# A graph-attention layer on one core: four ring buffers instead of five, and a twelfth weight kept in SBUF

## The chip, the core and the metric

The kernel runs on one core of one Trainium2 chip. Its time is the device time of one execution in microseconds (us). The kernel before took 2680.55 us, the median of three runs (2680.24 to 2683.42). One more execution was profiled; all rows below come from it.

## What is computed

The reference is one attention layer over 128 graphs of 128 nodes with 768 features, in float32, with 12 heads of 64:

```
h = relu(layernorm(x))                      # x: (128, 128, 768)
q, k, v = h @ Wq + bq, h @ Wk + bk, h @ Wv + bv
s = q k^T / sqrt(64) + beta * adj           # per head, adj: (128, 128, 128)
s = where(adj > 0, s, -9e15)
out = x + softmax(s) v
```

Most of the arithmetic is the three projections, 768 x 768 each, over 16,384 rows.

## The kernel before, in words

**Groups and slices.** The work runs in 32 groups of four graphs (`GRP = 4`). A group has three slices, in this order: `qk0` (the first half of the columns of Wq and Wk), `v` (Wv), and `qk1` (the other half of Wq and Wk). In groups 1 to 31 a slice is not computed as plain block products: the blocks go through a fast matrix multiplication with 15 products (table `PRODUCTS`), and each product is again seven 128x128 products instead of eight. `product` (line 662) issues one of them: 7 zones, each in two column halves, 28 TensorE matmul records of line 679 in the trace and as many weight loads. So a group is 45 products. This text numbers them as **slots 0 to 44**: 0 to 14 are `qk0`, 15 to 29 are `v`, 30 to 44 are `qk1`. The order inside a slice is a written list (`ORDER`; group 1 and the last group have lists of their own). The scores (line 774) and the attention products (line 853) of earlier slices are put between the slots by a table of due times (`TABLE`), and so are the evictions and decodings on VectorE, ScalarE and GpSimd (`EVICT`, `DECODE`).

**Prepared weights.** Each slot multiplies with a prepared weight: sums and differences of weight blocks, a tile of 128 x 7 x 128 floats, 448 KB. The 45 prepared weights are the same for all groups. Eleven of them stay in SBUF as tiles named `res_...` (`RESIDENT`, line 119, gives their slots: 0, 3, 16, 17, 19, 28, 29, 35, 38, 39, 42). The other 34 are written to DRAM once (`kept_...`, line 387) and read back in every group from 1 to 31 into a ring of `RING = 5` buffers (tag `T`, tiles `T_qk`, `T_v`).

**The ring.** `load_T` (line 433) issues one read on SyncE's queue (SP). At the end of each streamed slot, `product` calls it once (line 683). It takes the buffer that this slot has just freed, so the DMA waits, on SP, for the slot's last matmul. With five buffers the read that waits for one streamed slot brings the weight of the fifth streamed slot after it. SP works in order: everything behind a waiting read waits too. The same queue carries the loads of x (`x`, `xo`, `sbig`), of `adj`, and the output.

**Group 0.** The first group has no prepared weights yet. `plain_slice` (line 1027) computes its slices with ordinary block products, from raw weights in `sbig`. Beside it `prepare` (line 365) makes the 45 prepared weights step by step: `sums` on VectorE, and `finish` with `rest` on VectorE and GpSimd, which ends with the store to DRAM. `home(name)` (line 367) chooses where a weight is made: in its own tile if it is resident; else, for `qk0` and `v`, by a running count (`made_in`): the counts 2, 5 and 7 of every eight go to a buffer of the tag `e` (three buffers, later used for the scores), the others to the ring's tag `T`. The non-resident weights of `qk1` all go to `T`. A buffer can be taken again only when its store has landed. The ring is then filled ahead of group 1: two `load_T` in the middle of the `qk1` preparation (line 417) and `RING - 2` more at lines 1316 and 1317.

**Blocks.** Eight more tiles `home0` to `home7` (line 644) hold projections while they are summed up. In group 0 the first six serve `qk0`; the other two are first written by the first row of `qk1`.

Of the kernel before, what the change touches and what calls it, by code (L numbers as in the profile page):

```python
# [11 lines left out]
F32 = mybir.dt.float32  # L12
# [6 lines left out]
P = 128  # L19
# [12 lines left out]
@with_exitstack  # L32
def kernel(
    ctx: ExitStack,
    tc: tile.TileContext,
    x: bass.AP,
    adj: bass.AP,
    wq: bass.AP,
    bq: bass.AP,
    wk: bass.AP,  # L40
    bk: bass.AP,
    wv: bass.AP,
    bv: bass.AP,
    beta: bass.AP,
    out: bass.AP,
):

    nc = tc.nc
    keep = ctx.enter_context(tc.tile_pool(name="keep", bufs=1))
    bad = keep.tile([1, 1], I32, name="bad")
    args = (x, adj, wq, bq, wk, bk, wv, bv, beta, out)
    direct(tc, *args, bad)
    again = nc.values_load(bad[0:1, 0:1])
    with tc.If(again > 0):
        general(tc, *args)  # L60
# [54 lines left out]
PORDER = (1, 0, 5, 2, 3, 10, 7, 6, 13, 11, 4, 9, 14, 8, 12)  # L115
XORDER = (1, 0, 5, 2, 3, 10, 6, 7, 13, 11, 4, 9, 14, 8, 12)
ORDER = {"qk0": (1, 0, 5, 2, 10, 3, 6, 7, 13, 11, 9, 4, 14, 12, 8), "v": (1, 0, 5, 2, 10, 3, 6, 7, 13, 11, 4, 9, 14, 8, 12), "qk1": (4, 1, 0, 8, 2, 3, 5, 6, 7, 10, 9, 13, 11, 12, 14)}
RING = 5
RESIDENT = (0, 3, 16, 17, 19, 28, 29, 35, 38, 39, 42)
EB = 3  # L120
HOMES = 8

# [103 lines left out]
def direct(ctx, tc, x, adj, wq, bq, wk, bk, wv, bv, beta, out, bad):  # L226
# [25 lines left out]
    const = ctx.enter_context(tc.tile_pool(name="const", bufs=1))  # L252
# [104 lines left out]
    sequence = [(sl, n) for sl in ("qk0", "v", "qk1") for n in ORDER[sl]]  # L357
    resident = {key: const.tile([P, 7, P], F32, name=f"res_{key[0]}_{key[1]}") for key in (sequence[at] for at in RESIDENT)}
    kept, tz = {}, {}
    made_in = [0]  # L360

    def quarters(t):
        return t[:, 0:6].rearrange("p (c z) n -> p c z n", c=2)[:, :, 0:2]

    def prepare(sl):

        def home(name):
            n = [i for i, p in enumerate(PRODUCTS) if p[1] == name][0]
            if (sl, n) in resident:
                return resident[sl, n]  # L370
            made_in[0] += sl != "qk1"
            if sl != "qk1" and made_in[0] % 8 in (2, 5, 7):
                t = work.tile([P, 2, W], F32, tag="e", name=f"prep_{sl}_{n}", bufs=EB)
                return t.rearrange("p i w -> p (i w)")[:, 0:7 * P].rearrange("p (z n) -> p z n", n=P)
            return work.tile([P, 7, P], F32, tag="T", name=f"prep_{sl}_{n}", bufs=RING)

        def rest(n, t, b11, b12, b22, b=None):
            nc.vector.tensor_tensor(t[:, 6], b12, b11, ALU.subtract)
            nc.vector.tensor_tensor(t[:, 2], b22, b12, ALU.add)
            if b is not None:  # L380
                nc.gpsimd.tensor_copy(t[:, 0:2], b[:, 0])
                nc.gpsimd.tensor_copy(t[:, 3], b[:, 1, 0])
            nc.gpsimd.tensor_tensor(t[:, 4], t[:, 1], t[:, 6], ALU.add)
            nc.gpsimd.tensor_tensor(t[:, 5], t[:, 0], t[:, 4], ALU.subtract)
            if (sl, n) not in resident:
                k = kept[sl, n] = dram.tile([P, 7, P], F32, name=f"kept_{sl}_{n}")
                nc.sync.dma_start(k, t)

        made = {}

        def sums(name):
            for out, a, b, sign in SUMS_B:
                if out == name:
                    if out not in made:
                        made[out] = home(out)
                    at = [quarters(made[q]) if q in made else wt[sl, q] for q in (a.strip("-"), b)]
                    op = ALU.add if sign > 0 else ALU.subtract
                    if a[0] == "-":
                        nc.vector.scalar_tensor_tensor(quarters(made[out]), at[0], -1.0, at[1], op0=ALU.mult, op1=op)
                    else:  # L400
                        nc.vector.tensor_tensor(quarters(made[out]), at[0], at[1], op)  # L401

        def finish(name):
            n = [i for i, p in enumerate(PRODUCTS) if p[1] == name][0]
            if name in made:
                t = made[name]
                rest(n, t, t[:, 3], t[:, 4], t[:, 1])
            else:
                t, b = home(name), wt[sl, name]
                rest(n, t, b[:, 1, 0], b[:, 1, 1], b[:, 0, 1], b)  # L410

        steps = []
        for first, then_finish in PREPARED:
            for name in first:
                steps.append(lambda name=name: sums(name))
            if sl == "qk1" and first[0] == "T0":
                steps += [load_T, load_T]
            for name in then_finish:
                steps.append(lambda name=name: finish(name))
        return steps  # L420
# [12 lines left out]
    def load_T():  # L433
        if nt[0] < len(ring):
            G, sl, n = ring[nt[0]]
            nt[0] += 1
            t = tz[G, sl, n] = work.tile([P, 7, P], F32, tag="T", name=f"T_{G}_{sl}_{n}", bufs=RING)
            nc.sync.dma_start(t, kept[sl, n])
# [202 lines left out]
        while between and next(between[0], None) is None:  # L641
            between.popleft()

    homes = deque(const.tile([P, 7, P], F32, name=f"home{i}") for i in range(HOMES))
    home_of = {}

    def home_qk(G, sl, r, j, zones=False):
# [542 lines left out]
    def then(at, f, *args):  # L1190
        todo.setdefault(at, []).append(lambda: f(*args))
# [6 lines left out]
    def bias(G, *at):  # L1198
        for n in at:
            then(n, bias_step, G)  # L1200
# [114 lines left out]
    bias(1, 4, 6, 8)  # L1315
    for n in range(2, RING):
        then(10 + n, load_T)
# [29 lines left out]
    while events:  # L1347
        _, _, f, args = heapq.heappop(events)
# [149 lines left out]
```

## Time and profile before

| what | value |
|---|---|
| median of three runs | 2680.55 us |
| profiled execution, its own time | 2681.86 us |
| its span, first to last instruction | 2680.1 us |
| granted TensorE clock, mean | 0.997 |
| busy share of the span: PE, VectorE, ScalarE, GpSimd | 99%, 81%, 66%, 78% |
| data moved by DMA | 721.95 MB, 269 GB/s on average |
| reads from the ring's DRAM copies | 744 + 310 = 1054 of 448 KB |

The busy share of PE counts pipelined matmuls whose ends are modelled, so what an idle stretch costs is read from the waits, the timeline and the chain of waits instead. In the timeline a row gives the start in us from the span's start, the length in us, the engine, the line of the kernel, the operation, what it writes and reads, its shape, and how many instructions are merged; a bracket gives the idle time before it and what ended it. A row of line 679 with x28 is one slot, with x56 two slots. In the view of waits a row gives who waited for whom, the sum in us, how often, and the longest. `issue` stands for a wait that no event in the profile explains.

### The profile page before, as it was taken

What the parts mean: (1) busy time and instruction counts of PE and PEld (TensorE: products, weight loads), DVE (VectorE), ACT (ScalarE), POOL (GpSimd) and SP (SyncE); (2) the same over time, 40 slices, a digit from 0 to 9 for tenths busy, and PEclk for the clock granted to TensorE, in tenths of its full rate; (3) what the DMA queues carried; (4) which work ended last, traced back from release to release, by engine and by line L of the source; (5) the groups of instructions that cost most, each with busy time, mean ns of one, the idle gap of its engine ahead of it and who ended that gap; (6) DMA issues with size and microseconds to landing.
All of it is one profiled execution on the core that took longest, in us unless ns stands there. A gap on an engine that the chain in (4) does not pass through costs nothing.

```text
span 2680.1 us, 121170 instructions
## 1 busy us (share of the span) xinstructions
PE 2648.6 (99%) x52041; PEld 2569.4 (96%) x52041; DVE 2180.8 (81%) x2702; ACT 1756.8 (66%) x4608; POOL 2095.4 (78%) x3043
## 2 busy tenths in 40 slices
PE   9999999999999999999999999999999999999998
PEld 8799999999999999999999999999999999999997
DVE  7878888878888888888788888788888778777886
ACT  2567766676766677666677666777666766657654
POOL 5877778877778877878777788777788777887775
PEclk9999999999999999999999999999999999999999
DMA  8799898899989989989989999898999889888875
GB/s 250 257 284 279 271 279 276 270 283 270 276 278 274 278 279 268 285 273 269 284 271 274 277 279 276 274 273 272 283 274 275 264 247 283 271 266 263 244 253 171
DMA packets 526962, 721.95 MB, mean 269 GB/s; under 512 B 105932, under 2 KB 370648, under 8 KB 526424
## 3 DMA queue, kind: packets, MB, share of 16 engines
q1 hardware_dynamic: 525776, 713.38, 87.6%
q8 instruction: 411, 6.73, 1.0%
q14 instruction: 127, 1.04, 0.1%
q10 hardware_dynamic: 648, 0.79, 0.1%
HBM read 647.99 MB, written 66.05 MB: 266 GB/s over the span
## 4 chain that ended last, share of the span: by engine, by line
PE 91%; DMA 3%; DVE 2%; ACT 1%; issue 1%; SPq 1%; POOL 0%; ACTq 0%; DVEq 0%
PE pair L679 78%; PE pair L774 7%; PE pair L853 6%; DMA x<-in_x_dram 1%; DMA T_qk<-kept_qk 1%; DMA sbig<-in_L_gnn_Wk_dram 1%; PE pair L1046 1%; DVE prep_qk L401 0%; SPq L334 0%; SPq L597 0%; ACT x L558 0%; DVE home L702 0%; DMA kept_qk<-prep_qk 0%; DVE e L787 0%; ACT sbig L521 0%
## 5 line engine op out<-in xcount | busy, mean ns | idle before, releaser
L702 DVE TENSOR_TENSOR home<-home,pair 128x896 f32<-128x896 f32 x824 | 870.7, 1076 | 201.2 <-PE pair L679 197.2
L679 PE MATMUL pair<-sbig,T_qk 128*64 128x128 f32 x13020 | 840.8, 273 | 2.4 <-DVE home L702 1.2
L679 PEld LDWEIGHTS pair<-sbig,T_qk 128*64 128x64 f32 x13020 | 712.2, 137 | 12.1 <-issue 6.8
L679 PE MATMUL pair<-A,T_qk 128*64 128x128 f32 x7812 | 521.2, 273 | 1.7 <-DMA T_qk<-kept_qk 1.0
L737 POOL TENSOR_TENSOR home<-home 128x256 f32<-128x256 f32 x301 | 241.5, 802 | 273.8 <-DVE home L702 273.6
L834 ACT ACTIVATE e<-e,sm 128x64 f32<-128x64 f32 x1512 | 381.4, 344 | 102.8 <-DVE sm L822 101.9
L679 PEld LDWEIGHTS pair<-A,T_qk 128*64 128x64 f32 x7812 | 429.9, 137 | 3.6 <-ACT home L724 1.4
L853 PE MATMUL pair<-v,e 128*64 128x65 f32 x6048 | 406.5, 221 | 0.0
L853 PEld LDWEIGHTS pair<-v,e 128*64 128x64 f32 x6048 | 365.0, 137 | 3.0
L679 PE MATMUL pair<-T_v,sbig 128*64 128x128 f32 x6076 | 365.3, 274 | 1.6 <-issue 1.0
L679 PEld LDWEIGHTS pair<-T_v,sbig 128*64 128x64 f32 x6076 | 340.0, 138 | 8.8 <-issue 8.0
L722 ACT ACTIVATE home<-pair 128x640 f32<-128x640 f32 x328 | 231.5, 706 | 117.5 <-PE pair L679 87.9
L740 POOL TENSOR_TENSOR home<-home 128x256 f32<-128x256 f32 x301 | 281.3, 934 | 23.6
L679 PE MATMUL pair<-sbig,res_qk 128*64 128x128 f32 x4340 | 287.6, 273 | 0.0
L738 POOL TENSOR_TENSOR home<-home 128x256 f32<-128x256 f32 x301 | 264.7, 879 | 23.6
L787 DVE SCALAR_TENSOR_TENSOR e<-pair,biasT 128x1024 f32<-128x1024 f32 x189 | 230.1, 1217 | 33.0 <-PE pair L774 33.0
L679 PEld LDWEIGHTS pair<-sbig,res_qk 128*64 128x64 f32 x4340 | 238.6, 137 | 5.5 <-issue 5.3
L558 ACT ACTIVATE x<-x,block 128x192 f32<-128x192 f32 x480 | 225.7, 540 | 6.9 <-DMA x<-in_x_dram 6.9
L796 ACT ACTIVATE e<-e 128x1024 f32<-128x1024 f32 x189 | 199.5, 1056 | 46.8 <-DVE e L787 42.6
L883 ACT ACTIVATE sm<-pair,tiny 128x8 f32<-128x8 f32 x189 | 50.4, 267 | 267.1 <-PE pair L853 267.1
L724 ACT ACTIVATE home<-pair,bqk 128x128 f32<-128x128 f32 x656 | 206.4, 375 | 0.0
L519 ACT ACTIVATE sbig<-sbig 128x768 f32<-128x768 f32 x116 | 98.4, 848 | 123.6 <-DMA sbig<-in_x_dram 123.6
(206 smaller groups left out, 4600.8 us busy)
## 6 DMA issues: line engine op xcount, KB each, us to landing
T_qk<-kept_qk SPq DMA_DIRECT2D x744, 448.0 KB, 4.8
T_v<-kept_v SPq DMA_DIRECT2D x310, 448.0 KB, 5.5
xo<-in_x_dram SPq DMA_DIRECT2D x190, 256.0 KB, 7.2
out_dram<-xo SPq DMA_DIRECT2D x189, 256.0 KB, 2.9
x<-in_x_dram SPq DMA_DIRECT2D x248, 192.0 KB, 7.2
sbig<-in_x_dram SPq DMA_DIRECT2D x116, 384.0 KB
kept_qk<-prep_qk SPq DMA_DIRECT2D x24, 448.0 KB, 3.5
adj<-in_adj_dram SPq DMA_DIRECT2D x128, 64.0 KB, 5.6
```

The lines of the kernel that those rows point to most:

```text
L558: nc.scalar.activation(t, t, AF.Relu, bias=shift[G, n], scale=rstd[G, n])
L679: nc.tensor.matmul(p[q:q + HD, at, :], lhs[:, q:q + HD], rhs, start=(first and at % 4 == 0), stop=True, skip_group_check=True)
L702: nc.vector.tensor_tensor(t, t, p[:, 0:7], op)
L722: nc.scalar.activation(t[:, 0:5], p[:, 0:5], AF.Copy, scale=float(sign))
L724: nc.scalar.activation(t[:, at], p[:, at], AF.Identity, bias=bqk[:, of, oc:oc + 1], scale=float(sign))
L737: e.tensor_tensor(t[:, 1:4:2], t[:, 1:4:2], twice(5), ALU.add)
L738: e.tensor_tensor(t[:, 2:5:2], t[:, 2:5:2], twice(1), ALU.add)
L740: e.tensor_tensor(t[:, 0:7:6], t[:, 0:7:6], twice(2), ALU.add)
L787: nc.vector.scalar_tensor_tensor(e[:, :, at], ps[:, :, at], SCORE_CAP * ISCALE, bias[:, :, at], op0=ALU.min, op1=ALU.add)
L796: nc.scalar.activation(e, e, AF.Exp, scale=1.0 / ISCALE)
L834: nc.scalar.activation(o[:, r, b, 0:HD], pa[:, r, b, 0:HD], AF.Copy, scale=t[:, 1, r, b:b + 1])
L853: nc.tensor.matmul(pa[q:q + HD, 2 * g + i, :], k[:, q:q + HD], vt[G, "v", r, h // 4][:, 4 * g + h % 4, :], start=True, stop=True, skip_gro ...
```

## The change

Three things change.

- `RING` is 4 instead of 5, so a read brings the weight of the fourth streamed slot after the one that frees its buffer.
- `RESIDENT` has twelve slots instead of eleven: 0, 11, 17, 19, 23, 26, 29, 35, 36, 38, 39, 42. Slots 11, 23, 26 and 36 become resident; slots 3, 16 and 28 become streamed. A group then streams 33 weights, not 34. The SBUF for the twelfth tile is that of the fifth buffer.
- In group 0, `home6` and `home7` are lent to the preparation of `qk0` and `v`: every fourth non-resident weight is made in one of them, in turn, instead of in the ring. For this the list of home tiles is made earlier in the program.

```diff
-RING = 5
-RESIDENT = (0, 3, 16, 17, 19, 28, 29, 35, 38, 39, 42)
+RING = 4
+RESIDENT = (0, 11, 17, 19, 23, 26, 29, 35, 36, 38, 39, 42)
...
     kept, tz = {}, {}
+    homes = deque(const.tile([P, 7, P], F32, name=f"home{i}") for i in range(HOMES))
+    lent = tuple(homes)[6:8]
     made_in = [0]
...
                 return t.rearrange("p i w -> p (i w)")[:, 0:7 * P].rearrange("p (z n) -> p z n", n=P)
+            if sl != "qk1" and made_in[0] % 4 == 0:
+                return lent[made_in[0] // 4 % 2]
             return work.tile([P, 7, P], F32, tag="T", name=f"prep_{sl}_{n}", bufs=RING)
...
-    homes = deque(const.tile([P, 7, P], F32, name=f"home{i}") for i in range(HOMES))
     home_of = {}
```

## The prediction

> **What bounds the kernel now.** I read the page first: the busy shares, the DMA queues, the issues.
>
> ```profile
> span 2680.1 us, 121170 instructions
> PE 2648.6 (99%) x52041; PEld 2569.4 (96%) x52041; DVE 2180.8 (81%) x2702; ACT 1756.8 (66%) x4608; POOL 2095.4 (78%) x3043
> ...
> q1 hardware_dynamic: 525776, 713.38, 87.6%
> q8 instruction: 411, 6.73, 1.0%
> ...
> T_qk<-kept_qk SPq DMA_DIRECT2D x744, 448.0 KB, 4.8
> T_v<-kept_v SPq DMA_DIRECT2D x310, 448.0 KB, 5.5
> ...
> kept_qk<-prep_qk SPq DMA_DIRECT2D x24, 448.0 KB, 3.5
> ```
>
> TensorE is idle for 2680.1 - 2648.6 = 31.5 us in all, and the data queue is 87.6% busy, so the question is which waits of TensorE the change makes or removes. Next the chain that ended last, in order of time. Its longest pieces repeat once a group:
>
> ```profile
> 253.51 12.62 PE pair L679 x228
> 334.52 12.62 PE pair L679 x228
> ...
> 2628.30 12.60 PE pair L679 x228
> ```
>
> A clean group takes 334.52 - 253.51 = 81.01 us. The 29 periods from the first row to the last take 2374.79 us, 81.89 each: 25.5 us over 29 clean ones. That is all that a better supply of TensorE could save in the groups. The view of waits says what holds TensorE there; first from 130 to 2640 us, then from 2070 to 2640 us, then what holds SyncE's queue:
>
> ```profile
> PE pair L679 <- issue: 12.6, 8, 3.4
> ...
> PE pair L679 <- DMA T_qk<-kept_qk: 1.0, 3, 0.4
> ```
>
> ```profile
> PE pair L679 <- issue: 11.6, 6, 3.4
> ```
>
> ```profile
> SPq L438 <- PE pair L679: 999.4, 713, 7.8
> ```
>
> The ring costs TensorE almost nothing now: 1.0 us, three times in the run. The larger item is "issue", and 11.6 of its 12.6 us fall into the last seven groups. The last row shows that a read waits on SyncE for its slot, 713 times: the reads go out as early as their buffer allows, and a ring one buffer shorter takes time from each of them.
>
> **The change part by part.**
>
> *Fewer reads.* 31 groups read 33 weights, not 34: 31 x 448 KB, 14.2 MB or 2% of the traffic. No transfer is on TensorE's path except by the 1.0 us above, so I book nothing; at best that 1.0 us goes. SyncE issues 31 times less, which nothing waits for. A resident weight multiplies as fast as a streamed one, so the swap costs TensorE nothing.
>
> *The shorter ring, slot by slot.* I take the group in which TensorE visibly waits for a weight: first its TensorE rows, then its SyncE rows.
>
> ```profile
> 417.06 3.23 PE L679 MATMUL pair<-T_v,sbig 128*64 128x128 f32 x56
> 420.12 3.25 PE L679 MATMUL pair<-res_v,A 128*64 128x128 f32 x56
> ...
> 424.73 3.23 PE L679 MATMUL pair<-sbig,T_qk 128*64 128x128 f32 x56
> 428.36 0.44 PE L679 MATMUL pair<-A,T_qk 128*64 128x128 f32 x4 [0.40 <-DMA T_qk<-kept_qk]
> ```
>
> ```profile
> 413.39 0.38 SPq L438 DMA_DIRECT2D T_qk<-kept_qk  x1
> 413.82 2.62 SPq L597 DMA_DIRECT2D adj<-in_adj_dram  x4
> 416.55 4.10 SPq L438 DMA_DIRECT2D T_qk<-kept_qk  x2
> ...
> 421.22 0.99 SPq L438 DMA_DIRECT2D T_qk<-kept_qk  x2
> ```
>
> ```profile
> 421.22 7.00 DMA T_qk<-kept_qk
> ```
>
> The TensorE rows are slots 26+27, 28+29, then 31+32 and the start of 33. The reads are those after slots 23, then (behind `adj`) 24 and 25, then 26 and 27. The chain's piece is the read after slot 26: it lands 7.00 us after its issue, at 428.22, and slot 33 waits 0.40 us for it.
> After the change slots 23 and 26 are resident and read nothing, and the read after slot 27 serves slot 32 instead of slot 34. How long a read occupies the queue I bound by the rates in two stretches of the table of windows, the second of which holds these reads:
>
> ```profile
> 395.00:406.00 11.00, 11.00 (x236) 10.66 (x234) 7.23 (x12) 6.80 (x17) 10.14 (x16) 1.00 1.05 309
> ...
> 413.00:430.00 17.00, 16.60 (x324) 16.00 (x322) 13.00 (x16) 8.78 (x20) 15.01 (x27) 1.00 0.96 312
> ```
>
> 448 KB at 312 GB/s is 1.5 us. With the queue that full the read after slot 27 lands 1.5 us behind 428.22, at 429.7 (an estimate from those rows). Two reads less ahead of it bring it 3.0 us forward, to 426.7. Slot 32 is the second half of the row at 424.73 and wants it at 426.3: it waits 0.4 us. The read after slot 28 is new; 1.5 us behind, it lands at 428.2, and slot 33 wants it at 427.96, so it adds nothing to a slot 32 that is already late. The read after slot 25 now serves slot 31 instead of 32: 1.5 us less time, one read less ahead of it, no change. So a group like this one, whose weight was late before, waits about as long as before, at slot 32. Most groups had no visible wait, and there slot 32 has some tenths of a us in hand.
>
> The other tight places: the read after slot 2 serves slot 6. In another group slots 1+2, 4+5 and 6 are
>
> ```profile
> 451.05 3.32 PE L679 MATMUL pair<-sbig,T_qk 128*64 128x128 f32 x56
> ...
> 457.78 3.23 PE L679 MATMUL pair<-sbig,T_qk 128*64 128x128 f32 x56
> 460.84 1.70 PE L679 MATMUL pair<-A,T_qk 128*64 128x128 f32 x28
> ```
>
> so it has 460.84 - 454.37 = 6.5 us. A slow one of these reads (the DMA issues of a narrow window) took
>
> ```profile
> T_qk<-kept_qk SPq DMA_DIRECT2D x1, 448.0 KB, 6.8
> ```
>
> so slot 6 waits 0 to 0.3 us. Slot 16 is streamed now, with the read after slot 12:
>
> ```profile
> 474.80 2.66 SPq L438 DMA_DIRECT2D T_v<-kept_v  x2
> ```
>
> ```profile
> 480.11 3.23 PE L679 MATMUL pair<-res_v,sbig 128*64 128x128 f32 x56
> ```
>
> 5.3 us against a median of 5.5, with slot 11's read gone from ahead of it: 0 to 0.2 us. The new read after slot 16 joins the busiest stretch (share 1.05 above), for slot 22, and is bounded by the same tenths.
> Per group: at least 0, since three groups alone wait now; at most the 0.3 + 0.2 + 0.4 named here and as much as 0.3 at slot 22, 1.2 us. I take 0.25, nearer to the lower end, because the medians of 4.8 and 5.5 us fit every window named but slot 16's: 30 groups x 0.25 = **+7.5 us** (-1.0 to +36).
>
> *Group 0.* With five ring buffers `qk1` starts with four sums (TX, T9, T12, T11) and finds a free fifth buffer for T2. With four, T2 needs T9's, whose store must have landed. VectorE's T2, SyncE's four `adj` issues and T9's store (the first of eight):
>
> ```profile
> 89.64 0.94 DVE L401 TENSOR_TENSOR prep_qk<-sbig 128x512 f32<-128x512 f32 x1
> ```
>
> ```profile
> 85.82 3.38 SPq L597 DMA_DIRECT2D adj<-in_adj_dram  x4
> 89.31 13.24 SPq L387 DMA_DIRECT2D kept_qk<-prep_qk  x8
> ```
>
> The store goes out at 89.31, held up by `adj`. The page's median landing of such a store is 3.5 us, the quickest one
>
> ```profile
> kept_qk<-prep_qk SPq DMA_DIRECT2D x1, 448.0 KB, 2.4
> ```
>
> so T2 starts at 91.7 to 92.8, 2.1 to 3.2 us late. Behind T2 on VectorE stand the other preparations and the transposed `adj`, for which ScalarE waits, and behind that the eviction for which TensorE waits:
>
> ```profile
> 101.43 0.72 ACT L607 ACTIVATE adj<-adj,beta_s 128x512 f32<-128x512 f32 x1 [6.09 <-DVE biasT L603]
> ```
>
> ```profile
> 103.02 4.11 PE L1046 MATMUL pair<-A,sbig 128*64 128x256 f32 x36 [1.38 <-ACT home L1063]
> ```
>
> TensorE already waits there, so no cover is left and the delay is passed on. The lent blocks work the other way: of the 23 non-resident weights of `qk0` and `v` 9 go to the ring instead of 14, 5 to the lent blocks. T1's wait for a store
>
> ```profile
> 43.16 2.28 DVE L401 TENSOR_TENSOR prep_qk<-prep_qk,sbig 128x512 f32<-128x512 f32 x3 [1.89 <-DMA kept_qk<-prep_qk]
> ```
>
> goes, and T10 in an `e` buffer is late next, on the same store: up to 1.3 us won, which VectorE gives back at its 3.79 us wait for the raw `qk1` weights:
>
> ```profile
> 83.25 1.00 DVE L401 TENSOR_TENSOR prep_qk<-sbig 128x512 f32<-128x512 f32 x1 [3.79 <-POOL prep_v L383]
> ```
>
> Moving the list of homes moves no instruction, and I book nothing for the loan: the two blocks are wanted again by the first evictions of `qk1`, of which the one before 103.02 is the second, and if the loan were not over by then, that eviction would be late as in the case of T2. Group 0: **+2.2 us** (-1.3 to +3.2).
>
> *The waits named "issue".* 411 packets of 16.4 KB on an instruction queue serve 104,082 matmuls and weight loads, one packet for 253 of them, through the same DMA engines as the data. I read the 11.6 us as TensorE waiting for code while the queue is full; the profile doesn't name it. The change takes slot 11's read out ahead of the full stretch and puts slot 16's into it. I take **0** (-11.6 to +11.6).
> The Trainium skill ("Runtime: NRT & Kernel Launch", section "Instruction fetch mechanics") says that code is refilled in 16 KiB blocks and that crossing a block is mostly hidden. The trace agrees on the size, 16.4 KB, and disagrees on the hiding if the 3.4 us wait is a fetch. By the rule this term is 0 with no range, and the third rival below falls away.
>
> **Sum.** 7.5 + 2.2 + 0 = +9.7 us on the profiled execution's 2681.86, 2691.6. The median of the runs is 1.3 us lower, so 2690 us.
>
> **The rivals.**
> *The ring is too short in every group.* If reads land like the late ones above, each group waits 1.0 us: 30 + 2.2, 2713 us. For it: the queue at 0.96 to 1.05 of its share where slots 16 to 33 are fed. Against it: three waits in 31 groups today. The Trainium skill ("Perfetto Trace Analysis", section "Optimization Strategy") takes the same gap repeated on the saturated engine as a sign of too few buffers; no repeated gap is in this trace, so by that rule the ring has a spare buffer now and says nothing on four.
> *Nothing measurable.* The new residents give back what the buffer takes, and T2's delay is all that is left: 2680 to 2685 us. For it: the balance at slots 31 and 32. Within 0.2% (5.4 us) a measurement of this kernel can't be told from no change.
> *Faster: the late groups get their code in time.* Place: behind slots 16 to 19 of the last seven groups. Price: 11.6 us, with the 1.0 us of weights 12.6; less group 0's 2.2, 2670 us. It decides when the ring's new waits stay below 10.4 / 30 = 0.35 us a group. For it: one read less ahead of that stretch. Against it: one more inside it, after slot 16.
>
> **How the numbers follow.** Forecast 0.39, short ring 0.12, nothing 0.20, code in time 0.29. The forecast's own range is 2686 to 2700. The range for all, 2666 to 2713, runs from the full "issue" gain to the short ring. Slower by over 0.2% is forecast and short ring, 0.51; same 0.20; faster 0.29.
>
> **What would show it.** Right: waits of slots 6, 16, 31 to 33 for `T_qk` or `T_v`, some 5 to 10 us in all; T2 in group 0 some 2 us after the slot it has now, and TensorE's 1.38 us wait grown to about 3.6. Wrong: 81.01 us in nearly all groups including the last seven (code in time), a bubble in every group (short ring), or T2 not waiting for the store.

## The result and the profile after

The changed kernel takes 2708.72 us, the median of six runs (2704.24 to 2719.57), against 2680.39 us for the kernel before on the same chip: a ratio of 1.012, with a 95% interval of 1.0095 to 1.0144 (the two medians alone give 1.0106, inside the interval). It is slower, by 28.3 us in the medians. The profiled execution took 2715.79 us, 33.9 us more than that of before; it lies 7.1 us above its own median and that of before 1.5 us, so some 5.6 of the 33.9 us are the choice of executions. The forecast was 2690.

First the page of the changed kernel, in the places quoted of before:

```profile
span 2714.0 us, 121159 instructions
PE 2661.0 (98%) x52041; PEld 2571.3 (95%) x52041; DVE 2183.4 (80%) x2702; ACT 1755.5 (65%) x4608; POOL 2075.2 (76%) x3043
...
q1 hardware_dynamic: 521168, 698.70, 85.0%
q8 instruction: 411, 6.73, 1.0%
...
PE 85%; DMA 8%; DVE 3%; ACT 1%; POOL 1%; issue 1%; SPq 0%; ACTq 0%; DVEq 0%; POOLq 0%
...
T_qk<-kept_qk SPq DMA_DIRECT2D x713, 448.0 KB
T_v<-kept_v SPq DMA_DIRECT2D x310, 448.0 KB
```

The traffic fell as computed (698.70 for 713.38 MB, which is 31 reads and one store of 448 KB), and the kernel is slower all the same. In the chain that ended last (the row that begins with PE 85%) 8% is now DMA. The same row of before:

```profile
PE 91%; DMA 3%; DVE 2%; ACT 1%; issue 1%; SPq 1%; POOL 0%; ACTq 0%; DVEq 0%
```

The view of waits says what TensorE waited for from 130 to 2640 us (sum in us, how often, the longest):

```profile
PE pair L682 <- DMA T_qk<-kept_qk: 14.1, 22, 1.6
PE pair L682 <- issue: 7.3, 9, 1.5
PE pair L682 <- DMA T_v<-kept_v: 3.4, 3, 2.3
...
PE pair L777 <- issue: 1.9, 2, 1.2
```

Line 682 of this kernel is line 679 of the one before, and line 777 (the scores) is line 774. Waits for weights were 1.0 us, three times; now they are 17.5 us, 25 times. The waits named issue fell from 12.6 to 9.2 us, both lines together. In the chain, in order of time, the long piece that repeats once a group no longer comes every 81.01 us:

```profile
419.96 12.62 PE pair L682 x228
502.48 12.62 PE pair L682 x228
584.88 12.62 PE pair L682 x228
```

The two periods are 82.52 and 82.40 us.

**Where the 33.9 us lie.** I took the start of each slot from the TensorE rows of both traces. Group 1 starts at 123.44, not 121.41 us: +2.0 us. Group 1 itself is 0.7 us shorter, groups 2 to 30 are 32.5 us longer, group 31 and the end 0.1 us. Of the 32.5 us (29 groups, 1.12 us each), the differences of the mean step from one slot's start to the next, times 29, put down to the slot that the step leads to:

| start of slot | us in 29 groups |
|---|---|
| 8 | +11.1 |
| 9 | +14.6 |
| 16 | +6.0 |
| 18 and 19 | +6.6 |
| 5 | +1.4 |
| 31 and 32, less 33 | +2.3 |
| 20 to 22 | -11.3 |
| all others | +1.8 |

The waits named issue lie in the rows of slots 18 to 22, -4.7 us together. So 25.7 us sit at slots 8 and 9, which the prediction did not name. Group 6 shows how. First TensorE's rows in the timeline (slots 3, 4 and 5; 6; scores; 7; the start of 8), then SyncE's, then the chain:

```profile
542.57 4.81 PE L682 MATMUL pair<-sbig,T_qk 128*64 128x128 f32 x84
547.21 1.70 PE L682 MATMUL pair<-A,T_qk 128*64 128x128 f32 x28
548.84 1.10 PE L777 MATMUL pair<-home 64*64 64x128 f32 x32
549.87 1.75 PE L682 MATMUL pair<-sbig,T_qk 128*64 128x128 f32 x28
552.44 0.44 PE L682 MATMUL pair<-sbig,T_qk 128*64 128x128 f32 x4 [0.82 <-DMA T_qk<-kept_qk]
```

```profile
544.36 1.85 SPq L442 DMA_DIRECT2D T_qk<-kept_qk  x2
546.30 0.38 SPq L515 DMA_DIRECT2D sbig<-in_x_dram  x1
546.74 0.42 SPq L909 DMA_DIRECT2D out_dram<-xo  x1
547.42 1.85 SPq L442 DMA_DIRECT2D T_qk<-kept_qk  x2
```

```profile
545.89 6.41 DMA T_qk<-kept_qk
```

The row of SyncE at 544.36 holds two reads, 1.5 us apart: the new one after slot 3, and the one after slot 4, issued at 545.89. With four buffers this second read brings the weight of slot 8 (with five it brought slot 9's). It lands 6.41 us after its issue, at 552.30, and slot 8 begins at 552.44.

Slot 9 is late in the same way. Its read is the first of the two at 547.42, just behind, and lands at 555.11; slot 9 begins at 555.25. A group earlier the chain itself goes through the read for slot 9 (issued at 464.90, landed at 472.49), and the row behind it is slot 9:

```profile
464.90 7.59 DMA T_qk<-kept_qk
472.62 1.97 PE pair L682 x32
```

In group 0 the first step of the prediction stands as forecast. VectorE's T2 row, SyncE's store of T9, and TensorE's row:

```profile
92.72 0.69 DVE L405 TENSOR_TENSOR prep_qk<-sbig 128x512 f32<-128x512 f32 x1 [2.69 <-DMA kept_qk<-prep_qk]
```

```profile
89.25 15.00 SPq L391 DMA_DIRECT2D kept_qk<-prep_qk  x8
```

```profile
105.05 4.11 PE L1049 MATMUL pair<-A,sbig 128*64 128x256 f32 x36 [2.27 <-ACT home L1066]
```

T2 starts at 92.72 and not at 89.64, because it waits for the store issued at 89.25, and TensorE's row starts 2.03 us later than the 103.02 of before. Its wait there grew from 1.38 to 2.27 us only, not to the 3.6 of the prediction, because TensorE arrives 1.1 us later: earlier in group 0 it now waits for VectorE's statistics, which it did not do before. The loan alone has such a wait too, 1.1 us.

```profile
PE pair L477 <- DVE st L466: 1.4, 1, 1.4
```

### The profile page after: what moved, and what is told of

Read it like the earlier page. It is cut to its first block, busy times and chain, and to the rows that moved or that the text cites. A ratio compares the mean times of both kernels' runs of the same rounds, so it can differ in the third digit from the quotient of the medians.

```text
span 2714.0 us, 121159 instructions
## 1 busy us (share of the span) xinstructions
PE 2661.0 (98%) x52041; PEld 2571.3 (95%) x52041; DVE 2183.4 (80%) x2702; ACT 1755.5 (65%) x4608; POOL 2075.2 (76%) x3043
## 3 DMA queue, kind: packets, MB, share of 16 engines
q1 hardware_dynamic: 521168, 698.70, 85.0%
## 4 chain that ended last, share of the span: by engine, by line
PE 85%; DMA 8%; DVE 3%; ACT 1%; POOL 1%; issue 1%; SPq 0%; ACTq 0%; DVEq 0%; POOLq 0%
PE pair L682 73%; PE pair L856 6%; PE pair L777 6%; DMA T_qk<-kept_qk 5%; DMA T_v<-kept_v 1%; PE pair L1049 1%; DVE home L705 0%; DMA sbig<-in_x_dram 0%; DMA kept_qk<-prep_qk 0%; ACT x L562 0%; DVE prep_qk L405 0%; DMA sbig<-in_L_gnn_Wk_dram 0%; ACT home L727 0%; DVE sbig L587 0%; ACT home L725 0%
## 5 line engine op out<-in xcount | busy, mean ns | idle before, releaser
L682 PE MATMUL pair<-A,T_qk 128*64 128x128 f32 x6944 | 470.4, 273 | 9.7 <-DMA T_qk<-kept_qk 5.8
L740 POOL TENSOR_TENSOR home<-home 128x256 f32<-128x256 f32 x301 | 236.9, 787 | 311.9 <-DVE home L705 311.9
L856 PE MATMUL pair<-v,e 128*64 128x65 f32 x6048 | 419.2, 221 | 0.0
L682 PEld LDWEIGHTS pair<-A,T_qk 128*64 128x64 f32 x6944 | 388.3, 137 | 13.8 <-issue 4.5
L856 PEld LDWEIGHTS pair<-v,e 128*64 128x64 f32 x6048 | 377.1, 137 | 3.0
L682 PE MATMUL pair<-T_v,sbig 128*64 128x128 f32 x5208 | 318.4, 274 | 8.8 <-DMA T_v<-kept_v 3.4
L725 ACT ACTIVATE home<-pair 128x640 f32<-128x640 f32 x328 | 231.4, 705 | 121.1 <-PE pair L682 91.3
L682 PEld LDWEIGHTS pair<-T_v,sbig 128*64 128x64 f32 x5208 | 291.0, 137 | 16.8 <-issue 9.8
L743 POOL TENSOR_TENSOR home<-home 128x256 f32<-128x256 f32 x301 | 270.8, 900 | 23.6
L682 PE MATMUL pair<-sbig,res_qk 128*64 128x128 f32 x4340 | 281.6, 273 | 0.0
L741 POOL TENSOR_TENSOR home<-home 128x256 f32<-128x256 f32 x301 | 263.2, 875 | 23.6
L682 PE MATMUL pair<-res_v,sbig 128*64 128x128 f32 x3472 | 215.9, 274 | 4.3 <-issue 4.3
L682 PE MATMUL pair<-T_v,A 128*64 128x128 f32 x3472 | 214.4, 274 | 0.1
```

The lines of the kernel that those rows point to most:

```text
L682: nc.tensor.matmul(p[q:q + HD, at, :], lhs[:, q:q + HD], rhs, start=(first and at % 4 == 0), stop=True, skip_group_check=True)
L725: nc.scalar.activation(t[:, 0:5], p[:, 0:5], AF.Copy, scale=float(sign))
L740: e.tensor_tensor(t[:, 1:4:2], t[:, 1:4:2], twice(5), ALU.add)
L741: e.tensor_tensor(t[:, 2:5:2], t[:, 2:5:2], twice(1), ALU.add)
L743: e.tensor_tensor(t[:, 0:7:6], t[:, 0:7:6], twice(2), ALU.add)
L856: nc.tensor.matmul(pa[q:q + HD, 2 * g + i, :], k[:, q:q + HD], vt[G, "v", r, h // 4][:, 4 * g + h % 4, :], start=True, stop=True, skip_gro ...
```

## The experiments

Ratios are against the kernel before, run beside each on the same chip, with 95% intervals. "Groups" is the time from the start of group 2 to the start of group 31 in the profiled execution: 2374.4 us before, 2406.9 changed. For comparison, the changed kernel's own ratio is 1.012 and its group 1 starts at 123.4 us.

**Each part alone.** The ring alone:

```diff
-RING = 5
+RING = 4
```

> The kernel before with RING = 4 and nothing else: the old eleven residents, 34 reads a group, no loan. Theory A (the missing buffer costs, through the short windows of slots 5 to 10): the window of slot 8 is the same as in the changed kernel, 5.6 us, because the same read, the one after slot 4, serves it. So slots 8 and 9 are late here too, and slots 24, 27, 31 to 34 with their windows of 6 to 8 us come on top: +30 to +50 us, 2710 to 2730. Theory B (the buffer is harmless, and the new residents cost, because slot 3 now has a read that goes out in front of the one for slot 8): slot 3 is resident here, so slot 8 is in time and the kernel loses at most 10 us, 2680 to 2690.

Measured: 2780.05 us, 1.0346 (1.0315 to 1.0376). Far outside both expectations. Group 1 starts at 134.6 us, 13.2 us late, and the groups take 83.8 us more. TensorE's waits from 130 to 2640 us:

```profile
PE pair L679 <- DMA T_v<-kept_v: 44.8, 55, 2.0
PE pair L679 <- issue: 25.2, 19, 2.7
...
PE pair L679 <- DMA T_qk<-kept_qk: 1.3, 5, 0.4
```

The weights of the slice `v` are late, those of `qk` hardly. Slot 27 alone costs 37 us (1.3 us more in the median group, a gap in nearly every group), slots 15, 25 and 26 together 25 us, and the starts of slots 18 to 20, where most waits named issue lie, 18 us. Slots 8 and 9 cost 2.2 us. So theory A was wrong on the place and B on the sum: the missing buffer costs much with the old residents, but in other slots. In the changed kernel slots 23 and 26, which are next to that place, are resident, and it costs nothing there.

The residents alone, eleven of the twelve:

```diff
-RESIDENT = (0, 3, 16, 17, 19, 28, 29, 35, 38, 39, 42)
+RESIDENT = (0, 17, 19, 23, 26, 29, 35, 36, 38, 39, 42)
```

> The kernel before with five buffers and eleven of the twelve new residents (slot 11 is left streamed, since a twelfth tile does not fit beside five buffers), no loan. Theory A (the missing buffer costs): the residents alone cost nothing; slots 8 and 9 have windows of 8 to 11 us and start in time; the waits named issue may shrink, as they did in the changed kernel: 2670 to 2682. Theory B (the choice of residents costs, at slots 3 to 9): slots 8 and 9 are late as in the changed kernel by 25 us in all: 2700 to 2710.

Measured: 2698.54 us, 1.0037 (1.0012 to 1.0062). Slots 8 and 9 start in time, as A says, but the time is not 2670 to 2682: group 1 starts 3.5 us later than before, and the groups take 10.3 us more, with +12.1 us at the start of slot 19 and smaller differences of both signs elsewhere. TensorE's wait there is named issue, and in sum it grew instead of shrinking; why, these runs do not settle:

```profile
PE pair L679 <- issue: 19.8, 19, 2.6
```

The loan alone (the diff shown above without its first two changed lines), twice, in two sets of runs:

> The kernel before with the loan of two blocks in group 0 and nothing else. My prediction booked the loan at nothing, with up to 1.3 us won on VectorE and given back, and the 2 us of group 0 to the fourth buffer: with five buffers T2 must not wait, group 1 must start at 121.4 as before, 2680 +- 3. Rival: the loan itself shifts the order of the stores, T2 waits here too, and group 1 starts at 123.4: 2682 +- 3.

> The loan alone with five buffers once more, beside the run before it on the same chip: 0.998 of before, 2677 to 2682, group 1 at 120.9. If the 0.2% of the first measurement was chance it is 1.000.

Measured: 2680.18 us, 0.998 (0.9962 to 0.9997), and 2679.38 us, 0.9985 (0.997 to 1.0). Group 1 starts at 120.9 and 121.1 us, 0.3 to 0.5 us earlier than before, and T2 does not wait. The ratios suggest 4 to 5 us, the second with an interval that reaches no change; the profiles show only those 0.3 to 0.5, and the rest I cannot place. Its waits named issue were 15.6 us in the one profile and 11.1 in the other, which is how much this item differs between two executions of one program.

The ring and the residents without the loan:

```diff
-            if sl != "qk1" and made_in[0] % 4 == 0:
-                return lent[made_in[0] // 4 % 2]
```

> The changed kernel without the loan: four buffers and the twelve new residents only. If the loan is what makes four buffers bearable in group 0, 14 weights of qk0 and v go through four buffers, VectorE waits for more stores, group 1 starts 3 to 8 us later than the 123.4 of the changed kernel, and the groups behind cost the same: 2712 to 2716. If the preparation has room, group 1 starts at 123.4 and the time is that of the changed kernel, 2708.

Measured: 2718.39 us, 1.0129 (1.0098 to 1.0161). Group 1 starts at 128.3 us, 4.9 us later than in the changed kernel, inside the 3 to 8 us expected. The groups behind, expected to cost the same, take 4.4 us more in this execution, and the time is above the 2712 to 2716 expected. TensorE waits longer at the same row of group 0:

```profile
108.21 5.79 PE L1047 MATMUL pair<-A,sbig 128*64 128x256 f32 x36 [4.72 <-ACT home L1064]
```

**Slots 8 and 9.** The changed kernel with slot 3 kept, slot 36 streamed:

```diff
-RESIDENT = (0, 11, 17, 19, 23, 26, 29, 35, 36, 38, 39, 42)
+RESIDENT = (0, 3, 11, 17, 19, 23, 26, 29, 35, 38, 39, 42)
```

> The changed kernel with one resident exchanged: slot 3 is kept again, slot 36 is streamed. Four buffers and the loan stay. The window of slot 8 (from the end of slot 4) is 5.6 us either way. Theory Q (slots 8 and 9 are late because the new read after slot 3 is queued just in front of the read for slot 8): the last packet for slot 8 comes 3.3 to 4 us after its release, not 5.5; the 25.7 us at slots 8 and 9 go; the time falls from 1.0105 of before to 1.000 to 1.003, about 20 us. Theory W (a window of 5.6 us is too short whatever is in front): slots 8 and 9 stay late, the time stays at 1.010 or so. Slot 36 has a window of over 7 us and should not be late under either.

Measured: 2702.5 us, 1.0089 (1.0065 to 1.0113). The place behaves as theory Q says. SyncE's timeline has one read there, and TensorE's slot 7 runs into slot 8 without a wait (28 + 4 matmuls in one row):

```profile
467.79 0.32 SPq L442 DMA_DIRECT2D T_qk<-kept_qk  x1
468.16 0.42 SPq L515 DMA_DIRECT2D sbig<-in_x_dram  x1
```

```profile
471.77 1.97 PE L682 MATMUL pair<-sbig,T_qk 128*64 128x128 f32 x32
```

Slots 8 and 9 together cost 2.2 us instead of 25.7, and the groups 23.9 us less than in the changed kernel. By the packet records of the two traces the last packet for slot 8 comes 5.5 us after its release in the median group of the changed kernel and 3.4 us here; the window is 5.6 us in both. Theory W falls. The whole time is 1.0089 of before, and not the 1.000 to 1.003 expected. Part of it is that group 0 became longer: group 1 starts at 128.2 us, 4.8 us later than in the changed kernel. The rest is scatter between executions or not explained: this profile lies 5.2 us below the median of its runs, that of the changed kernel 7.1 us above. The two ratios are only 0.3% apart, some 8 us, and their intervals overlap. So it is the place that shows the cause here, not the time. As I read the longer group 0, which was not tried alone: which weight is made in which buffer goes by a running count, so one exchanged resident moves all the weights behind it, and TensorE waits longer at the known row:

```profile
107.96 5.95 PE L1049 MATMUL pair<-A,sbig 128*64 128x256 f32 x36 [5.17 <-ACT home L1066]
```

With the first two runs the four combinations are complete. The late starts of slots 8 and 9 against the kernel before, in us over 29 groups:

| | slot 3 resident | slot 3 streamed |
|---|---|---|
| five buffers | 0 (before) | under 1 (residents alone) |
| four buffers | 2.2 (ring alone), 2.2 (slot 3 kept) | 25.7 (changed), 24.3 (changed, no loan), 30.4 (changed, T2 freed, below) |

Neither part alone does it. Taking the fifth buffer away shortens the window of slot 8, and the new read fills what is left of it. The trace also records when each read's completion is signalled (16 updates of its semaphore for every one of the reads; I take the last as its landing). In the median of groups 2 to 30, in us after the release:

| | window | read lands, changed | read lands, slot 3 kept |
|---|---|---|---|
| slot 8 | 5.6 | 5.7 | 3.7 |
| slot 9 | 6.5 | 7.2 | 6.0 |

So the new read puts off the two reads behind it, not only the next one. Slot 9 is late in 27 of 29 groups of the changed kernel, and in 26 of these it starts within 0.2 us of its own read's landing. The view of waits names the weight there in only eight of the 29 groups, so its 17.5 us for all weights understate what these two slots lose.

**Group 0.** The changed kernel with T2 taken out of the ring:

```diff
             made_in[0] += sl != "qk1"
+            if sl == "qk1" and name == "T2":
+                return lent[0]
```

> The changed kernel with T2 of qk1 in group 0 made in the first lent block, not in the ring, so that it needs no buffer that T9's store still holds. If that wait is what makes group 0 longer, as I predicted: T2's sums start at 89.6 us, not 92.7; TensorE's wait for ScalarE at 105 us falls from 2.3 to 1.4 us or less, and group 1 starts at 121.4 to 122, not 123.4. If the delay only moves to the eviction that wants the lent block next, or T2 was not the cause, group 1 starts at 123.4 again. The groups behind are those of the changed kernel: 2704 to 2718.

Measured: 2709.72 us, one run; group 1 starts at 125.0 us, 1.6 us later than in the changed kernel. T2 no longer waits, and the delay has moved, as the second half of the expectation says, to the eviction that wants the lent block. ScalarE's row, and TensorE's behind it:

```profile
97.66 0.84 ACT L1068 ACTIVATE home<-pair,bqk 128x256 f32<-128x256 f32 x2 [7.54 <-DMA kept_qk<-home]
```

```profile
98.55 5.36 PE L1051 MATMUL pair<-A,sbig 128*64 128x256 f32 x32 [2.31 <-ACT home L1068]
```

**The waits named issue.** Two sets of residents with five buffers and the loan, meant to take reads out from ahead of slots 15 to 19:

```diff
-RESIDENT = (0, 3, 16, 17, 19, 28, 29, 35, 38, 39, 42)
+RESIDENT = (0, 3, 14, 16, 17, 19, 28, 29, 35, 39, 42)       # first
+RESIDENT = (0, 3, 12, 14, 16, 17, 19, 28, 29, 35, 42)       # second
```

> Five buffers with the loan, eleven residents, those of the kernel before with slot 38 exchanged for slot 14, so that one read less goes out just ahead of slots 15 to 19. Theory F (the waits named issue at slots 17 to 19 are TensorE's code arriving late behind the reads in the DMA queue): with one read of 1.5 us less in front, waits of up to 3.8 us shrink by about 1.5 each, from the 15.6 us in sum of the loan alone to 4 to 8 us; 0.994 to 0.997 of before. Theory N (those waits are not code behind reads): they stay at 12 to 16 us, and the time is that of the loan alone, 0.998.

> As the run before it, with slot 12 resident too, in place of slot 39: two reads less ahead of slots 14 to 19. Theory F: the waits named issue at slots 17 to 19 go almost wholly, 0 to 4 us in sum; 0.992 to 0.996 of before, unless the run of eight streamed slots at the end of qk1 makes slots 1 to 6 late. Theory N: issue at 12 to 16 us, 0.998.

Measured: 2680.85 us, 0.9997 (0.9985 to 1.0008), and 2686.2 us, 1.001 (0.9995 to 1.0025). Both miss theory F's times, and neither settles it: issue is 14.2 us in the first and 11.7 in the second, within what two profiles of one program differ by. The second shows a price like that of its last clause, at other slots: with slots 36 to 44 all streamed but 42, slots 44 and 0 start 11 us late in all, with rows like

```profile
1763.82 1.75 PE L682 MATMUL pair<-sbig,T_qk 128*64 128x128 f32 x28 [1.60 <-DMA T_qk<-kept_qk]
```

Then one load of 384 KB moved, everything else as with the loan alone:

```diff
-    (-73.412, 'row', 2), (-67.751, 'row_stats', 2),
+    (-70.7, 'row', 2), (-67.751, 'row_stats', 2),
```

> The kernel before with the loan, and one load of 384 KB moved: the rows of x for the second graph pair's statistics are loaded at slot 19.3, not 16.6. Residents, ring and every read stay. Theory F (the waits named issue at slots 17 to 19 are code that arrives behind data in the DMA queue): 384 KB less in front of it is 1.2 to 1.3 us; waits of 0.7 to 3.8 us shrink by about that or go, from 15.6 us in sum to 5 to 9 us; 0.994 to 0.997 of before. Theory N (something else): 12 to 18 us as with the loan alone, 0.998. If the statistics come too late, ScalarE and the norms behind it show waits instead.

Measured: 2681.45 us, 0.9986 (0.997 to 1.0002), issue 14.7 us. No change: moving this load takes nothing off the waits. Then the larger one that is issued earlier, left out:

```diff
     def load_x(G, r):
+        if r == 1 and G >= 2:
+            xp[G, 1] = xp[G, 0]
+            for g in range(2):
+                xg[G, 2 + g] = xg[G, g]
+            return
         home_x(G, r)
```

> The loan alone with five buffers, and from group 2 on the second load of x in a group (four transfers of 192 KB, issued at slot 13.5) left out: the norms work on the first pair's rows again, so the output is wrong, while every instruction on the other engines stays. Theory F (the waits named issue at slots 17 to 19 are code that comes late behind data issued before it): 768 KB less in front of that stretch, some 2.5 us; no wait was longer than 3.8 us and most were under 2.5, so they nearly all go: issue below 5 us in sum, 0.993 to 0.996 of before. Theory N: issue stays at 11 to 16 us, and the time is that of the loan alone, 0.998.

Measured: 2662.42 us, 0.993 (0.9908 to 0.9952). The waits are gone but for 0.7 us:

```profile
PE pair L861 <- issue: 0.5, 2, 0.3
...
PE pair L687 <- issue: 0.2, 1, 0.2
```

The compute engines run as many instructions as before; only data in the DMA queue and its issues on SyncE were taken away, so theory F holds. The packet records fit: in the kernel before, the nine waits of over 0.4 us at slots 17 to 19 all end 1.3 to 1.9 us after a packet of 16.4 KB of the instruction queue has ended. The waits are also tied to a place in the code: in the kernel before they come inside slot 19, ahead of its matmul record 13, 16, 19, 22, 25 and 28 in groups 25 to 30, three records further in each group; in the changed kernel ahead of record 10, 16 and 19 in groups 24, 26 and 27, which is the same series.

**A version that beats both.** The same load kept, but issued two slots earlier, as soon as its buffer is free; five buffers, old residents, the loan:

```diff
-    (-31.526, 'load_x', 1),
+    (-33.3, 'load_x', 1),
```

> The loan with five buffers, and the second load of x (768 KB) not left out but issued at slot 11.7, not 13.5, as soon as the last transposition has read the buffer; in the loan's own profile that is some 2 us earlier (1370.4, not 1372.5 us). Output complete. If what is issued just before slots 15 to 19 is what makes the code late there, the waits named issue fall from 11 to 16 us to 3 to 8 us, and the time to 0.994 to 0.997 of before, better than both kernels. Rival: the queue is full from slot 12 on, so that the same bytes stand in front either way: issue 10 to 16 us, 0.998; and slot 15, whose last packet comes 2 us before its start now, may be late.

Measured: 2671.59 us, 0.9962 (0.9949 to 0.9974), 10 us under the 2681.61 us of the kernel before beside it; the changed kernel stands at 1.012 by the same measure. Against the loan alone (0.998 and 0.9985) it is some 0.2%, or 5 us. TensorE's waits from 130 to 2640 us:

```profile
PE pair L682 <- issue: 2.9, 5, 1.1
PE pair L777 <- issue: 2.4, 3, 1.0
PE pair L682 <- DMA T_qk<-kept_qk: 2.2, 3, 1.1
```

Its groups take 11.8 us less than with the loan alone, nearly all at the starts of slots 19 and 20. Slot 15 is not late.

## Why the prediction was right, and where it was wrong

The direction was right: slower, held most likely. The size was not: 2690 with an own range of 2686 to 2700, against 2708.72. The time lies inside the range for all, 2666 to 2713, only because that reached up to the rival of a short ring. By its steps:

- *Fewer reads*, 0: right as far as can be seen. 14.7 MB less brought no gain that shows.
- *The shorter ring, slot by slot*, +7.5 us: this is the term that failed, 32.5 us in groups 2 to 30. It failed by omission. Among the slots it named, 16 costs 6.0 us (0.2 a group, the upper end given), 31 to 33 cost 2.3, slots 6 and 22 nothing: 8.3 us, nearly the 7.5 booked. Slots 8 and 9 were not gone through, and they cost 25.7. The first row for it was quoted: slots 4 and 5 begin at 457.78, so slot 4 ends at 459.5. Two rows further on in TensorE's timeline of before stand slot 7 and the first four matmuls of slot 8:

```profile
463.50 1.97 PE L679 MATMUL pair<-sbig,T_qk 128*64 128x128 f32 x32
```

  Slot 8 starts at 465.1. That is a window of 5.6 us for the read after slot 4, shorter than the 6.5 us of slot 6, with a new read of 448 KB issued 1.5 us ahead of it. The sentence "the medians of 4.8 and 5.5 us fit every window named" took the landing times of before as if the reads in front stayed the same; with the new one in front slot 8's read landed 2.0 us later and slot 9's 1.2 us. Its upper bound of 1.2 us a group did hold the measured 1.12, but by luck: it was made of slots 6, 16, 22 and 32.
- *The balance at slots 31 to 33*: right in its outcome, +2.3 us. That the new residents 23 and 26 pay there is not shown: the ring alone, with the old residents, loses nothing there either (+2.0 at slot 32, -2.6 at slot 33). They pay at slots 25 to 27, which the prediction didn't cost: the ring alone loses 52 us there, the changed kernel nothing. In all groups it is 83.8 against 32.5.
- *Group 0*, +2.2 us: right in size (+2.0) and in its way (T2, the store behind `adj`, the eviction, TensorE), though TensorE's wait at that row grew by 0.9 us only. But "I book nothing for the loan" hid a balance: without the loan it is 6.9 us (group 1 at 128.3), of which the loan gives back 4.9; and the new residents alone cost 3.5 us there. So the right size is in part luck. The run with T2 freed shows that T2 is only the first of the steps that lack a buffer.
- *The waits named issue*, 0 (-11.6 to +11.6): -3.4 us by the view of waits, inside the bounds, and less than the 4.5 us by which two executions of the loan alone differ. The reading as late code was right, and the runs without and with the earlier load of x show it. The Trainium skill ("Runtime: NRT & Kernel Launch", section "Instruction fetch mechanics") calls the crossing of a 16 KiB block mostly hidden. Here 411 packets are fetched, and TensorE waits eight times in the kernel before and 11 times in the changed one, up to 3.4 us each; with 768 KB less data ahead three waits are left, of 0.3 us at most.
- *The rivals.* The short ring in every group named 1.0 us a group and 2713 us; the time came out near it, 1.12 us a group, with slots 8 and 9 in place of the slots 16 to 33 for which it argued. It was given 0.12, too little. The Trainium skill's sign of too few buffers, the same gap again and again on the saturated engine ("Perfetto Trace Analysis", section "Optimization Strategy"), shows where the ring alone was shortened: 1.3 us at slot 27 in the median group. Code in time did not win: the issue waits fell by 3.4 us, not 11.6, and the ring's new waits were above the 0.35 us a group at which it decided. Nothing measurable is excluded: the interval begins at 1.0095, 25 us above no change.

## What to carry to other kernels

When a ring loses a buffer, list the window of every streamed slot (from the end of the slot that frees its buffer to its own start), not only of those that are late today, and add to the landing time each read that is newly issued just ahead of it (1.5 us here); look at the second read behind the new one too. A resident paid here where it took a read out from in front of a short window, and its choice and the depth of the ring have to be priced together. Where an engine waits for "issue" while the queue is full, try moving the largest transfer issued just before that stretch.

## What the runs showed of the hardware

- A read of 448 KB issued 1.5 us ahead of another put the latter's landing off by 2.0 us (from 3.7 to 5.7 us after its release, medians at slot 8; by the last packet from 3.4 to 5.5 us), more than the 1.5 us that its bytes take at the 312 GB/s of a full stretch. The read behind that one landed 1.2 us later (6.0 to 7.2 us, slot 9).
- A slot that waits for its read starts 0.13 us after the last of the read's 16 completion updates (medians of slots 8 and 9 in the changed kernel and of 15 and 27 with the ring alone). Packets put to reads in the order of their start show less: by them slot 8 had 0.8 us left and slot 9 2.1 us, while both were late.
- TensorE's code comes in packets of 16.4 KB, and TensorE waits for it when data is queued ahead: the waits named issue were 15.6 and 11.1 us in two executions of the loan alone, 0.7 us with 768 KB a group left out, and 26.1 us with the ring alone. They differ by 4.5 us between two profiled executions of one program, so they may be part of the scatter between runs; that was not tried.
